# First layer's up projections by seven products of quarters

## The chip, the cores and the metric

The kernel runs on one core of a Trainium2 chip. A core has five engines that work through their own instruction queues in order and wait for each other by semaphores: TensorE (PE in the profile, with its weight loads as PEld), VectorE (DVE), ScalarE (ACT), GpSimd (POOL) and SyncE (SP, which issues most transfers). PE multiplies matrices and writes to PSUM banks; the other engines read PSUM or SBUF; POOL works on SBUF alone. The metric is the device time of one execution in microseconds; lower is better.

## The reference

The reference computes two layers on x of shape (2, 512, 512). Cut to what matters here:

```python
# layer 0, on xn = layernorm(x)
f = rfft(xn); corr = irfft(f * conj(f))            # autocorrelation of each row
weights, delay = top_k(corr, 6); w = softmax(weights)
s = sum over the 6 of w * xn rotated by delay
h = relu(xn @ up_w) ** 2                           # 512 -> 1024: the up projection
shared = h @ down_w                                # 1024 -> 512
routed = ((xn @ fc1_w) @ expert_w) * (sum of top 2 of xn @ gate_w) @ fc2_w
g = silu(layernorm(shared + routed) * gamma + beta)
x = x + s * g
# layer 1: a state-space mixer with 128 heads, and a gated feed-forward from int4 weights
```

Layer 0 is about a tenth of the time; everything that the change touches lies in it.

## The kernel before

Each of the two batches is a 512 x 512 block. Its normalized rows are transposed, so that `xnT` holds features in partitions (128 partitions, 4 blocks k of features) and the 512 rows in the free dimension. For each batch b layer 0 runs these stages, which line numbers of the profile name:

- `spectrum` (L222): the halves' sum `xu` and difference `xv` (L228 on DVE, L229 on POOL; for batch 0 row by row at L267 and L268), four spectra `xf` on PE (L235), copies on DVE (L243), squares on ACT (L245), the sum of two squares on DVE (L248).
- for b = 1 the `epilogue` of batch 0 (L334): layer norm of `ff`, product with gamma on POOL (L341), sum with beta on DVE (L342), SiLU on ACT (L343), product with the aggregate on POOL (L344), update of `x1` on DVE (L345), a store issued by POOL (L346).
- the up projection, `up_to` (L357). It makes the eight tiles of h, each 128 of the 1024 outputs by 512 rows: four matmuls over k into one PSUM bank `hu` (L361), ReLU on ACT (L369), square on POOL (L370). For b = 1 three tiles are written ahead of the correlations, the other five behind them.
- the correlations `corr`, four row blocks r (L388), and for each block the softmax over the six largest: halves (L379 to L381), maximum (L399), its negation (L401), exponentials on ACT (L404, L412, L413), match-replace (L409), the difference `w` on POOL (L415), its scaling on DVE (L416), and the halves `wuv` on POOL (L418, L419).
- `xl` (L432), the transposes of the lags' weights into `wT` (L444), their spectra `wf` (L454) and products, the router and the routed part (L483, L496), the aggregate `ag` (L507), and the down projection `sh` (L522).

A Python program writes all this with a layer that tracks dependencies and sets the semaphores. Outside of the blocks marked as scheduled by hand, a scheduler orders the instructions of layer 0 on each engine. Every engine then keeps that order: an instruction that isn't ready holds up what stands behind it. Buffers go by tags. A tag with one buffer is given to the next tile when the last reader of the former is done: `xu`, `xv` and `wT` are such tags. The PSUM banks `mm` are six, taken in turn, so a seventh tile waits until the first is read out. The weights `up_sb` lie in a ring of six buffers; the loads for the second layer's first weights (L643, L644, multiplied at L647) take these buffers when they come free.

The second layer has its order written by hand. It already uses seven products in place of eight for its projections: `row_sums` (L572), `column_sums` (L564), `seven` (L586) and `product` (L603), whose matmuls all have the line L607.

Of the kernel before, what the change touches and what calls it, by code (L numbers as in the profile page):

```python
# [8 lines left out]
F32 = mybir.dt.float32  # L9
I32 = mybir.dt.int32  # L10
AF = mybir.ActivationFunctionType
ALU = mybir.AluOpType
# [3 lines left out]
P = 128  # L16
D = 512
B = 2
S = 512
T = B * S  # L20
KD = D // P
HD = D // 2
# [26 lines left out]
def fused_kernel(  # L49
# [31 lines left out]
    nc = tc.nc  # L81
# [32 lines left out]
    def ring(name, dtype=F32):  # L114
        return wring.tile([P, 4, 512], dtype, tag="w", name=name)


    hand = early.enter_context(tc.tile_pool(name="hand", bufs=1, side="right"))
# [6 lines left out]
    def bank(name, shape=(P, 512)):  # L125
        return epsum.tile(list(shape), F32, tag="mm", name=name, bufs=6)

    def features(src, dst, name):

        pt = epsum.tile([P, KD, P], F32, tag="tr", name=name, bufs=2)  # L130
        for k in range(KD):
            nc.tensor.transpose(pt[:, k, :], src[:, bass.ts(k, P)], ident)
        nc.scalar.copy(dst, pt)

    def second_features(b):

        t = hand.tile([P, KD, S], F32, tag=f"xnT{b}", name=f"xn1T{b}")
        for r in range(NCH):
            rt = b * NCH + r
            features(acc[rt], t[:, :, bass.ts(r, P)], f"xn1t{rt}")  # L140
        return t

    x1s = ExitStack()
    x1p = x1s.enter_context(tc.tile_pool(name="x1", bufs=1, side="right"))
# [5 lines left out]
    with ExitStack() as l0:  # L150
        keep = l0.enter_context(tc.tile_pool(name="l0", bufs=1, side="left"))
# [12 lines left out]
        first = (0, HD, 1, HD + 1)  # L164
# [8 lines left out]
        up_sb = []  # L173
        for h in range(2):
            t = ring(f"up{h}")
# [10 lines left out]
        for h in range(2):  # L186
            t = ring(f"dn{h}")
# [28 lines left out]
        def halved(b):  # L216

            return [
                keep.tile([P, 2, S], F32, tag=tag, name=f"{tag}{b}") for tag in ("xu", "xv")
            ]  # L220
# [69 lines left out]
        with tc.manual_schedule():  # L290
            mv = keep.tile([P, NCH, 2], F32, tag="mv", name="mva0", bufs=2)
            rs = keep.tile([P, NCH], F32, tag="rs", name="rsa0", bufs=2)
            xu, xv = halved(0)
# [40 lines left out]
        def epilogue(b, fl, ags):  # L334

            mv, rs = stats(fl, f"f{b}")
            for r in range(NCH):
                rt = b * NCH + r
                f = fl[r]
                normed(f, f, mv, rs, r)  # L340
                nc.gpsimd.tensor_tensor(f, f, gam, ALU.mult)  # L341
                nc.vector.tensor_tensor(f, f, bet, ALU.add)  # L342
                nc.scalar.activation(f, f, AF.Silu)  # L343
                nc.gpsimd.tensor_tensor(f, f, ags[r], ALU.mult)  # L344
                nc.vector.tensor_tensor(x1[rt], x1[rt], f, ALU.add)  # L345
                nc.gpsimd.dma_start(x1_d[rows(rt), :], x1[rt])  # L346
# [3 lines left out]
        for b in range(B):  # L350
            xnT = xnTs[b]
            xf, sq = spectra.pop() if spectra else spectrum(b)
            if rest:
                epilogue(b - 1, *rest)
            h_sb = []

            def up_to(n, b=b, xnT=xnT, h_sb=h_sb):  # L357
                for o in range(len(h_sb), n):
                    ps = bank(f"hu{b}{o}")
                    for k in range(KD):  # L360
                        nc.tensor.matmul(  # L361
                            ps,
                            up_sb[o // 4][:, k, bass.ts(o % 4, P)],
                            xnT[:, k, :],
                            start=(k == 0),
                            stop=(k == KD - 1),
                        )
                    h = hand.tile([P, S], F32, tag=f"h{o}", name=f"h{b}_{o}")
                    nc.scalar.activation(h, ps, AF.Relu)  # L369
                    nc.gpsimd.tensor_tensor(h, h, h, ALU.mult)  # L370
                    h_sb.append(h)

            if rest:
                up_to(3)

            def halves(dst, ps, name):

# [7 lines left out]
            for r in range(NCH):  # L385
                ps = bank(f"corr{b}{r}")
                for c in range(3):
# [4 lines left out]
                        start=(c != 1),  # L392
                        stop=(c != 0),
# [20 lines left out]
                w = keep.tile([P, D], F32, tag="w", name=f"w{b}_{r}", bufs=2)  # L414
# [14 lines left out]
            for o in range(2):  # L429
                ps = bank(f"xl{b}{o}")  # L430
                for k in range(KD):
# [4 lines left out]
                        start=(k == 0),  # L436
                        stop=(k == KD - 1),
                    )
                nc.vector.tensor_copy(xl[:, o, :], ps)
            if b > 0:  # L440
                xn1T.append(second_features(b - 1))


            wT = keep.tile([P, KD, S], F32, tag="wT", name=f"wT{b}")  # L444
# [3 lines left out]
            for lo in range(2):  # L448
                wf = {}
                re, im = 2 * lo, 2 * lo + 1  # L450
                for c in (re, im):
                    ps = bank(f"wf{b}{c}")
                    for k in range(2):
# [4 lines left out]
                            start=(k == 0),  # L458
                            stop=(k == 1),
# [19 lines left out]
            for r in range(NCH):  # L479
                rt = b * NCH + r  # L480
                pl = bank(f"lg{rt}", (P, 8))
                for k in range(KD):
# [4 lines left out]
                        start=(k == 0),  # L487
                        stop=(k == KD - 1),
# [10 lines left out]
                f = keep.tile([P, D], F32, tag=f"ff{r}", name=f"ff{rt}")  # L499
# [3 lines left out]
            for r in range(NCH):  # L503
                rt = b * NCH + r
                ps = bank(f"ag{rt}")
                for c in range(4):
# [4 lines left out]
                        start=(c % 2 == 0),  # L511
                        stop=(c % 2 == 1),
# [4 lines left out]
            for r in range(NCH):  # L517
                rt = b * NCH + r
                f = fl[r]
                pd = bank(f"sh{rt}")  # L520
                for o in range(INT0 // P):
# [4 lines left out]
                        start=(o == 0),  # L526
                        stop=(o == INT0 // P - 1),
# [29 lines left out]
    hT = mix.tile([P, KD, T], F32, tag="hT", name="hT")  # L557
    th = mix.tile([P, B, 4, 2, HD], F32, tag="th", name="th")

    def column_quarters(a):  # L560

        return [a[:, 2 * k : 2 * k + 2, bass.ts(j, HD)] for k in range(2) for j in range(2)]

    def column_sums(b, a):  # L564


        b11, b12, b21, b22 = column_quarters(a)
        t1, t2, t3, t4 = (th[:, b, i] for i in range(4))
        for dst, p, q in ((t1, b12, b11), (t2, b22, t1), (t3, b22, b12), (t4, b21, t2)):
            nc.gpsimd.tensor_tensor(dst, p, q, ALU.subtract)  # L570

    def row_sums(a, s1, s2, s3, s4):  # L572

        a11, a12, a21, a22 = row_quarters(a)
        for dst, p, q, op in (
            (s1, a21, a22, ALU.add),
            (s2, s1, a11, ALU.subtract),
            (s3, a11, a21, ALU.subtract),
            (s4, a12, s2, ALU.subtract),
        ):  # L580
            nc.gpsimd.tensor_tensor(dst, p, q, op)  # L581

    def row_quarters(a):
        return [a[:, 2 * k : 2 * k + 2, bass.ts(r, P)] for r in range(2) for k in range(2)]

    def seven(a, sums, columns, b):  # L586


        a11, a12, _, a22 = row_quarters(a)
        s1, s2, s3, s4 = sums  # L590
        b11, _, b21, b22 = column_quarters(columns)
        t1, t2, t3, t4 = (th[:, b, i] for i in range(4))
        return {
            1: (a11, b11),
            2: (a12, b21),
            3: (s4, b22),
            4: (a22, t4),
            5: (s1, t1),
            6: (s2, t2),
            7: (s3, t3),  # L600
        }

    def product(ps, factors, first):  # L603

        x, y = factors
        for k in range(2):
            nc.tensor.matmul(  # L607
                ps,
                x[:, k, :],
                y[:, k, :],  # L610
                start=(first and k == 0),
                stop=(k == 1),
                skip_group_check=True,
            )

    Dcol = mix.tile([P, DIN // P], F32, tag="Dcol", name="Dcol")
    cw = mix.tile([P, (DIN + 2 * NG * NST) // P, KCONV], F32, tag="cw", name="cw")
# [18 lines left out]
    with ExitStack() as l1:  # L636
# [225 lines left out]
        def pair_of_tiles(its, sums, b, name):  # L862


            f = {kind: seven(*sums[kind], xn1T[b], b) for kind in "gu"}
            ps = {kind: bank(f"p{kind}{name}", (P, 2, HD)) for kind in "gu"}
            us = {
# [6 lines left out]
            def multiply(kind, i, y=None):  # L874
                if i == 2:
                    product(y, f[kind][i], kind == "g")
                else:
                    product(ps[kind][:, int(i in (3, 5))], f[kind][i], i == 1)
# [74 lines left out]
        w = {"g": fin["g"](), "u": fin["u"]()}  # L953
# [7 lines left out]
        sums = ahead = {}  # L961
        for n, (i0, iw) in enumerate(blocks):
# [13 lines left out]
            for q, b in order:  # L976
                two, name = its[b][2 * q : 2 * q + 2], f"{i0}{q}{b}"
# [24 lines left out]
                if b == 1:  # L1002
                    sums = ahead
# [9 lines left out]
            for b in range(B):  # L1013
                for r in range(NCH):
                    rt = b * NCH + r
                    po = bank(f"pf{i0}{rt}")
                    for i in range(ni):
# [4 lines left out]
                            start=(i == 0),  # L1022
                            stop=(i == ni - 1),
# [26 lines left out]
    with ExitStack() as sm:  # L1050
# [9 lines left out]
        sums, rgs = {}, {}  # L1060
# [264 lines left out]
        class Values:  # L1325
# [3 lines left out]
            def __init__(self, s):  # L1329
                self.s = s  # L1330
                u, g, b, t, h0 = place(s)
                self.ct = g * GT + t
                w = whs[s // 2]
                self.factors = seven(w, pair_sums(w, "sh", s), hT[:, :, bass.ts(b, S)], b)
                self.ps = {}

            def multiply(self, *which):
                for i in which:
                    tile = int(i not in (2, 3))
                    if i in (1, 2):  # L1340
                        self.ps[tile] = psum.tile(
                            [P, 2, HD], F32, tag="pj", name=f"pjh{self.s + tile}", bufs=3
                        )
                    product(self.ps[tile][:, int(i in (3, 5))], self.factors[i], i in (1, 2))

            def quarter(self, i, j):
                return hid[self.s + i][:, bass.ts(j, HD)]
# [657 lines left out]
```

## Time and profile before

| | us |
|---|---|
| median of 3 runs (2237.49 to 2237.68) | 2237.58 |
| the profiled execution's own time | 2236.23 |
| its span, first to last instruction | 2234.2 |
| `hu` of batch 0 in the chain, 64 passes | 27.47 |
| `hu` of batch 1 in the chain, 24 + 40 passes | 10.30 + 17.17 |
| layer 1's first product begins | 225.36 |
| L607, two products (8 passes of 256 columns) | 1.73 |

A float32 matmul is two passes in the profile. A row of the timeline gives the start, the busy time, the engine, the line, the operation, the tile written and the tiles read, the shapes, how many instructions were merged (x8), and in brackets the idle time of the engine before it and what ended that. A row of the chain gives the start, the length, the engine, the tile and the line. The granted clock of PE was 0.998 over the span.

### The profile page before, as it was taken

To read this page: it belongs to the slowest core of one execution; us is meant where nothing else is said; L and a number is where in the kernel's file an instruction comes from. 1 tells how busy PE (TensorE), PEld (TensorE's weight loads), DVE (VectorE), ACT (ScalarE), POOL (GpSimd) and SP (SyncE) were. 2 spreads that over 40 slices of the span, in tenths; PEclk is the share of its full clock that TensorE was granted. 3 is DMA by queue.
4 is the path that set the end of the run, shared out by engine and by line. 5 is a ranking of instruction groups with operands and counts; after the bars stand their busy time and mean duration, and the time that the engine had idled before them with its cause. 6 is when DMAs were issued, how large, how long until landed. Compare 5 with 4: busy or idle time off the path is not lost.

```text
span 2234.2 us, 35459 instructions
## 1 busy us (share of the span) xinstructions
PE 2198.2 (98%) x12460; PEld 1716.8 (77%) x12460; DVE 1524.5 (68%) x2989; ACT 1297.1 (58%) x2864; POOL 1311.8 (59%) x1224
## 2 busy tenths in 40 slices
PE   8999999999999999999999999999999999999997
PEld 4545567765578888888888888888888888888876
DVE  5273577545777777777767777777777777777753
ACT  4131323214876767676767676766767676767650
POOL 4151533323566667766866585768667766866485
PEclk9999999999999999999999999999999999999999
DMA  4021266755644545344544444454545444544442
GB/s 172 1 68 65 96 227 217 245 193 189 188 144 132 160 131 166 123 133 130 180 144 148 156 135 123 133 178 131 154 138 171 123 132 123 183 136 144 158 127 95
DMA packets 195521, 323.51 MB, mean 145 GB/s; under 512 B 17680, under 2 KB 129168, under 8 KB 192912
## 3 DMA queue, kind: packets, MB, share of 16 engines
q1 hardware_dynamic: 188944, 300.28, 43.2%
q0 software_dynamic: 6400, 20.98, 2.4%
q8 instruction: 99, 1.62, 0.3%
q14 instruction: 78, 0.64, 0.1%
HBM read 294.45 MB, written 26.74 MB: 144 GB/s over the span
## 4 chain that ended last, share of the span: by engine, by line
PE 82%; DVE 8%; ACT 7%; issue 2%; DMA 0%; POOL 0%; SPq 0%; ACTq 0%; POOLq 0%; DVEq 0%
PE of L1527 13%; PE pjh L607 12%; PE gt L607 11%; PE pjbc L1139 4%; PE py L1177 4%; PE pf L1018 4%; PE py L1186 3%; PE pn L1276 3%; PE hu L361 2%; PE sh L522 2%; PE pg L607 2%; PE px L1230 2%; PE pu L607 2%; PE gt L1139 2%; PE gty L607 2%
## 5 line engine op out<-in xcount | busy, mean ns | idle before, releaser
L1301 POOL TENSOR_TENSOR eb<-CT,eb 128x768 f32<-128x768 f32 x128 | 230.2, 1820 | 339.4 <-DMA eb<-ea_d 255.5
L1254 ACT ACTIVATE cs<-cs,sl 128x128 f32<-128x128 f32 x1024 | 325.2, 391 | 0.2 <-DMA cs<-cs_d 0.2
L1158 DVE SCALAR_TENSOR_TENSOR hid<-pjh,cw,hid 128x511 f32<-128x511 f32 (+2 forms) x384 | 286.6, 746 | 42.3 <-ACT hid L1149 34.8
L1269 DVE TENSOR_TENSOR cs<-de,CB 128x512 f32<-128x512 f32 x256 | 175.5, 686 | 80.4 <-ACT de L1268 79.6
L1655 POOL TENSOR_TENSOR y<-y,sgt 128x512 f32<-128x512 f32 x124 | 175.4, 1435 | 14.8 <-ACT sgt L1410 11.8
L1177 PE MATMUL py<-cs,hc 128*64 128x128 f32 x2048 | 181.4, 277 | 0.0
L1268 ACT ACTIVATE de<-cs 128x512 f32<-128x512 f32 x256 | 154.0, 602 | 28.7 <-DVE cs L1269 22.6
L1222 POOL TENSOR_TENSOR sums<-sums,sq 128x512 f32<-128x512 f32 x110 | 140.2, 1274 | 39.4 <-ACT sq L1218 35.7
L1289 DVE SCALAR_TENSOR_TENSOR st<-st,sl,pn 128x64 f32<-128x64 f32 x512 | 108.4, 275 | 77.3 <-ACT st L1285 77.3
L1186 PE MATMUL py<-eb,st 128*64 128x128 f32 x1536 | 149.9, 274 | 0.0
L1541 DVE SCALAR_TENSOR_TENSOR acc<-of,rg,acc 128x256 f32<-128x256 f32 x192 | 92.4, 482 | 81.7 <-PE of L1527 80.8
L1177 PEld LDWEIGHTS py<-cs,hc 128*64 128x64 f32 x2048 | 122.4, 138 | 19.9 <-issue 18.1
L1206 DVE SCALAR_TENSOR_TENSOR y<-hid,Dcol,y 128x512 f32<-128x512 f32 x128 | 133.7, 1045 | 4.5
L1354 ACT COPY hid<-pjh 128x256 f32<-128x256 f32 x171 | 63.4, 371 | 126.5 <-PE pjh L607 125.9
L581 POOL TENSOR_TENSOR sw<-wg 128x256 f32<-128x256 f32 x57 | 42.2, 740 | 153.0 <-PE gt L607 152.9
L1205 DVE TENSOR_TENSOR y<-py,el 128x512 f32<-128x512 f32 x128 | 87.8, 686 | 58.5 <-PE py L1186 57.8
L1399 ACT COPY sgt<-gt 128x256 f32<-128x256 f32 x171 | 64.0, 374 | 103.1 <-PE gt L607 102.8
L607 PE MATMUL gt<-th,wg 128*128 128x256 f32 x456 | 118.7, 383 | 4.2 <-DVE sgt L1403 4.2
L1527 PE MATMUL of<-wt,y 128*128 128x256 f32 x512 | 121.3, 380 | 0.0
L607 PE MATMUL pjh<-th,wh 128*128 128x256 f32 x456 | 118.7, 383 | 1.8 <-ACT hid L1354 1.8
L1139 PE MATMUL pjbc<-hT,wbc 128*128 128x512 f32 x256 | 117.4, 593 | 2.1 <-DVE BT L1158 1.3
L1527 PE MATMUL of<-wo,s 128*128 128x256 f32 x496 | 117.9, 381 | 1.2 <-DVE acc L1541 1.2
(353 smaller groups left out, 5548.6 us busy)
## 6 DMA issues: line engine op xcount, KB each, us to landing
cs<-cs_d SPq DMA_DIRECT2D x128, 512.0 KB, 4.1
eb<-ea_d SPq DMA_DIRECT2D x256, 192.0 KB, 6.0
wh<-in_in_wT SPq DMA_DIRECT2D x64, 512.0 KB, 9.0
wg<-in_in_wT SPq DMA_DIRECT2D x64, 512.0 KB, 7.3
el<-ea_d SPq DMA_DIRECT2D x256, 128.0 KB, 7.5
wo<-wo_d SPq DMA_DIRECT2D x16, 1024.0 KB, 8.2
wop<-in_out_wT SPq DMA_DIRECT2D x39, 256.0 KB, 2.8
wo_d<-wop POOLq DMA_DIRECT2D x39, 256.0 KB, 2.8
```

The lines of the kernel that those rows point to most:

```text
L607: nc.tensor.matmul(ps, x[:, k, :], y[:, k, :], start=(first and k == 0), stop=(k == 1), skip_group_check=True,)
L1139: nc.tensor.matmul(ps, w_of(k), hT[:, k, bass.ts(b, S)], start=(k == 0), stop=(k == KD - 1))
L1158: nc.vector.scalar_tensor_tensor(dst[:, j:], ps[:, : S - j], cw[:, ct, KCONV - 1 - j : KCONV - j], dst[:, j:], ALU.mult, ALU.add,)
L1177: nc.tensor.matmul(py[bass.ts(hh, HP), bass.ts(c, P)], hc[:, c, bass.ts(hh, HP)], M[:, hh, bass.ts(c, P)], start=True, stop=(c == 0),)
L1186: nc.tensor.matmul(py[bass.ts(hh, HP), bass.ts(c, P)], st[:, c - 1, bass.ts(hh, HP)], cte[:, hh, bass.ts(c - 1, P)], start=False, stop=True,)
L1222: nc.gpsimd.tensor_tensor(sums[u], sums[u], q, ALU.add)
L1254: nc.scalar.activation(m[:, bass.ts(c, P)], m[:, bass.ts(c, P)], AF.Relu, bias=sls[g][:, 3, b * NCH + c, h0 + hh : h0 + hh + 1], scale=-1.0,)
L1268: nc.scalar.activation(pe, m, AF.Exp, scale=-1.0)
L1269: nc.vector.tensor_tensor(m, pe, CBs[s // GT].rearrange("p c i -> p (c i)"), ALU.mult)
L1301: nc.gpsimd.tensor_tensor(eb_t[s], CTs[s // GT][:, P:].unsqueeze(1).to_broadcast([P, 2, S - P]), eb_t[s], ALU.mult,)
L1527: nc.tensor.matmul(ps, x[:, k, :], y[:, k, :], start=(first and k == 0), stop=(k == 3), skip_group_check=True,)
L1655: nc.gpsimd.tensor_tensor(y_of(s), y_of(s), sgs.pop(s), ALU.mult)
```

## The change

Two tiles of the up projection are made together, as one product of 2 x 2 quarters. The weights of the two tiles (512 features by 256 outputs) are cut into quarters of 256 features by 128 outputs, `xnT` into quarters of 256 features by 256 rows. Four sums of weight quarters (`row_sums`, on POOL) and four differences of quarters of `xnT` (`difference_sums`, on POOL, once a batch) let seven products of quarters stand for the eight. The differences lie in the buffers of `xu` and `xv`, the row sums in that of `wT`, with room for two pairs.

The seven are named by number: 1 is (a11, b11), 2 is (a12, b21), 3 is (s4, b22), 4 is (a22, t4), 5 is (s1, t1), 6 is (s2, t2), 7 is (s3, t3). They accumulate in two halves of one bank (`ps`) and one bank of their own (`py`); ACT copies partial sums out between products, and DVE adds the rest. ReLU now reads SBUF. Ahead of batch 1's correlations one pair (two tiles) is written in place of three tiles. The functions are moved to the top, and layer 1 calls them with its own sums as before.

```diff
+    def difference_sums(t, columns):
+        b11, b12, b21, b22 = column_quarters(columns)
+        t1, t2, t3, t4 = t
+        for dst, p, q in ((t1, b12, b11), (t2, b22, t1), (t3, b22, b12), (t4, b21, t2)):
+            nc.gpsimd.tensor_tensor(dst, p, q, ALU.subtract)
...
-            def up_to(n, b=b, xnT=xnT, h_sb=h_sb):
-                for o in range(len(h_sb), n):
-                    ps = bank(f"hu{b}{o}")
-                    for k in range(KD):
-                        nc.tensor.matmul(
-                            ps,
-                            up_sb[o // 4][:, k, bass.ts(o % 4, P)],
-                            xnT[:, k, :],
-                            start=(k == 0),
-                            stop=(k == KD - 1),
-                        )
-                    h = hand.tile([P, S], F32, tag=f"h{o}", name=f"h{b}_{o}")
-                    nc.scalar.activation(h, ps, AF.Relu)
-                    nc.gpsimd.tensor_tensor(h, h, h, ALU.mult)
-                    h_sb.append(h)
+            def up_to(n, b=b, xnT=xnT, h_sb=h_sb, tus=tus, sws=sws):
+                if not h_sb:
+                    for q, tag in enumerate(("xu", "xv")):
+                        t = keep.tile([P, 2, 2, HD], F32, tag=tag, name=f"tu{b}_{q}")
+                        tus.extend(t[:, i] for i in range(2))
+                    difference_sums(tus, xnT)
+                    sws.append(keep.tile([P, 2, 4, 2, P], F32, tag="wT", name=f"su{b}"))
+                for o in range(len(h_sb), n, 2):
+                    w = up_sb[o // 4][:, :, bass.ds(o % 4 * P, 2 * P)]
+                    sw = [sws[0][:, o // 2 % 2, i] for i in range(4)]
+                    row_sums(w, *sw)
+                    fs = seven_of(w, sw, xnT, tus)
...
+                    ps, py = bank(f"hu{b}{o}", (P, 2, HD)), bank(f"huy{b}{o}", (P, HD))
...
+                    product(ps[:, 0], fs[1], True)
+                    product(ps[:, 1], fs[5], False)
+                    product(py, fs[2], True)
+                    nc.scalar.copy(quarter(0, 0), ps[:, 0])
+                    nc.vector.tensor_tensor(quarter(0, 0), quarter(0, 0), py, ALU.add)
+                    product(ps[:, 0], fs[6], False)
+                    nc.scalar.copy(quarter(0, 1), ps[:, 0])
+                    product(ps[:, 0], fs[7], False)
+                    nc.scalar.copy(quarter(1, 1), ps[:, 0])
+                    nc.vector.tensor_tensor(quarter(1, 1), quarter(1, 1), ps[:, 1], ALU.add)
+                    product(ps[:, 0], fs[4], False)
+                    product(ps[:, 1], fs[3], False)
+                    nc.scalar.copy(quarter(1, 0), ps[:, 0])
+                    nc.vector.tensor_tensor(quarter(0, 1), quarter(0, 1), ps[:, 1], ALU.add)
+                    for h in hs:
+                        nc.scalar.activation(h, h, AF.Relu)
+                        nc.gpsimd.tensor_tensor(h, h, h, ALU.mult)
+                        h_sb.append(h)
 
             if rest:
-                up_to(3)
+                up_to(2)
```

## The prediction

> **What bounds the kernel now.** I read the page first (busy shares, the chain that ended last), then the chain in order of time over the first 330 us, then the timelines of PE, POOL, DVE and ACT there.
>
> ```profile
> span 2234.2 us, 35459 instructions
> PE 2198.2 (98%) x12460; PEld 1716.8 (77%) x12460; DVE 1524.5 (68%) x2989; ACT 1297.1 (58%) x2864; POOL 1311.8 (59%) x1224
> PE 82%; DVE 8%; ACT 7%; issue 2%; DMA 0%; POOL 0%; SPq 0%; ACTq 0%; POOLq 0%; DVEq 0%
> ```
>
> PE is busy 98% of the span, and the chain is PE for 82%. So PE time that goes is worth its full length only where PE still waits for nobody.
>
> ```profile
> 30.45 1.73 PE corr L388 x8
> 32.18 27.47 PE hu L361 x64
> 59.64 6.87 PE xl L432 x16
> ...
> 128.33 10.30 PE hu L361 x24
> 138.63 5.18 PE corr L388 x24
> 143.81 17.17 PE hu L361 x40
> ...
> 269.92 1.73 PE pg L607 x8
> ```
>
> In the chain both up projections (hu) stand whole, without a gap: 64 passes in 27.47 us (0.429 each, 512 columns), and in the second batch 24 passes ahead of the correlations (corr) and 40 behind. The other engines' rows that matter:
>
> ```profile
> 31.27 2.36 POOL L229 TENSOR_TENSOR xv<-xnT 128x1024 f32<-128x1024 f32 x1 [12.97 <-ACT xnT L133]
> 43.42 1.04 POOL L370 TENSOR_TENSOR h<-h 128x512 f32<-128x512 f32 x1
> 250.19 1.27 POOL L570 TENSOR_TENSOR th<-xn1T,th 128x512 f32<-128x512 f32 x1
> 263.13 0.74 POOL L581 TENSOR_TENSOR sg<-w_g,sg 128x256 f32<-128x256 f32 x1
> ```
>
> ```profile
> 35.88 0.49 DVE L416 TENSOR_SCALAR w<-w,zs 128x512 f32<-128x512 f32 x1 [0.37 <-POOL w L415]
> 43.49 1.28 DVE L416 TENSOR_SCALAR w<-w,zs 128x512 f32<-128x512 f32 x1 [0.62 <-POOL w L415]
> 133.50 0.68 DVE L248 TENSOR_TENSOR sq<-sq,sq 128x512 f32<-128x512 f32 x1
> ```
>
> ```profile
> 39.77 0.30 ACT L404 ACTIVATE e<-m,nm 128x6 f32<-128x6 f32 x1 [2.21 <-DVE m L407]
> 276.00 0.37 ACT L881 COPY it<-pg 128x256 f32<-128x256 f32 x1 [2.22 <-PE pg L607]
> ```
>
> The reader is to see two things. The same DVE scaling takes 0.49 us with POOL idle and 1.28 where a POOL square runs from 43.42 to 44.46: it ends about 0.3 us after the square. So a DVE operation that works from SBUF alone waits for a POOL operation in flight, and the other way round; DVE rows that read PSUM (the 0.68 us copies at L243 beside POOL) don't. And ACT idles 2.21 us for the softmax of row block 2, which costs nothing now, since PE needs nothing from ACT in that stretch.
>
> **The change part by part.**
>
> *Fewer columns on PE.* A pair of tiles was 16 passes of 0.429 = 6.87 us; it becomes seven products of 4 passes of 256 columns, and L607's rows give 1.73 per 8, so 7 x 0.864 = 6.05. Eight pairs (four per batch): 8 x 0.82 = 6.6 us off PE.
>
> *More on the others.* Per pair four row sums on POOL (0.73, pitch 0.69), four copies on ACT (0.37), three DVE adds from PSUM (0.41, L885's rows), and ReLU from SBUF (0.63 as at L343, for 0.59). Per batch four difference sums on POOL (1.27, pitch 1.23). In all 2 x (16 x 0.69 + 4 x 1.23) = 32 us POOL, about 10 ACT, 8 DVE. No engine becomes the bound by its total. What counts is the place: three of seven products write a bank that ACT must have copied and DVE must have read, and ACT, DVE and POOL do their instructions strictly in the written order. I took that order from the changed program and walked the queues with the durations above, each DVE operation from SBUF waiting for POOL's in flight. The same walk of the kernel before starts hu at 31.9 (trace 32.0), the second hu at 127.9 (128.2) and the second layer's first product at 224.9 (225.4).
>
> *Ahead of hu, batch 0.* POOL now has eight row sums (from 18.3, when xv ends and the first half of up_w has landed) and four differences, to about 29.9. Inside that stretch DVE has the sum of squares (L248) and the four normalizations that feed the transposes which stand before hu. Two of them take 1.7 us instead of 0.5; PE waits 1.2 and 1.2 at the transposes: +2.4.
>
> *Inside hu, batch 0.* Product 7 of pair 0 needs ACT's copy of product 6. On ACT that copy stands behind the exponentials of row block 2, these wait for DVE's negated maximum, which stands behind the scaling of row block 1, which waits for POOL's subtraction at 40.2 to 41.5, itself behind a row sum of pair 2. PE is through at 40.6 and goes on at 43.0: +2.4. Then product 4 waits for DVE's add of 7 and 5, behind the scaling of row block 2 (POOL, 45.5 to 46.8): +2.0. Smaller waits +0.9. Batch 0: +7.7 - 3.3 = +4.4.
>
> *Batch 1, first wait.* Before, three hu tiles (10.3 us) covered the sum of squares, done at 134.2. Now three products (2.6 us) and two corr products stand there, so PE arrives at 135.8. The sum stands on DVE behind the epilogue of batch 0. The differences can only start when xf has read the halves whose buffers they take; two of them stand on POOL ahead of the gamma products, two more and a row sum behind these, and DVE's additions and normalization alternate with them. The walk gives 142.8: +7.0.
>
> *Batch 1, second wait.* Product 4 of pair 0 needs DVE's add into h1, queued behind the four updates of x, the last of which waits for POOL's product behind a SiLU. PE is through at 148.0, goes on at 153.9: +5.9. Three further waits, for a bank that DVE's corr halves free (2.2), an ACT copy (0.9 with the neighbour) and DVE's add of pair 1 (1.9): +5.0. Batch 1: +18.0 - 3.3 = +14.7; then about 0.3 at the later transposes.
>
> *Moved.* Batch 1's halves xu and xv (2.20 and 2.36 us, L228, L229) go from 31-35 to behind batch 0's differences, about 61; xf reads them at 121, sixty microseconds of cover. The loads of w_g and w_u wait for up_w's last readers: w_g was issued at 147.3, now about 175, w_u 164.8, now about 185 (landing about 7.4 later). Their DVE products stand before two h adds (read by sh at 217) and before the multiplications at wf (about 195, read by ag at 210): nothing, with some 5 us of cover on the latter; without it ag waits. SP's other issues are not moved against each other.
>
> *Clock.* Two idle gaps of 7.0 and 5.9 us are new; in the trace PE, once started, never idles more than about 1 us, so no row shows what follows such a gap. The nearest are the first 7 us: transposes x8 1.94 against 1.04, ext and exf likewise at about half rate, together 3.4 us lost. Bounds 0 to 3.4 each. I take 0, because PE then runs into waits that DVE and ACT end. The Trainium skill (TensorE: Matmul & The Clock Gate, "What's actually happening") speaks against the change here: after an idle window of some 3.4 us the clock is halved until PE has been busy as long. By that the sum would be 1.7 larger per gap, up to 22.8 in place of 19.4; no row of this trace shows it.
>
> *Sum.* +4.4 + 14.7 + 0.3 = +19.4. The profiled execution took 2236.2 (span 2234.2 and 2.0 around it), so 2255.6; the median of the three runs shown, 2237.58, lies 1.35 above, so **2257.0**. Behind layer 0 PE's order is unchanged and without slack, so nothing is given back. With POOL rows 10% shorter the walk gives 18.2, 20% longer 22.5; with up_w's half landing at 19 instead of 17, 20.1.
>
> **The rivals.**
>
> *The sums hide, PE gets its gain.* Place: the wait of product 7 and 4 on ACT and DVE. If the copies were answered before PE has done the other pair's products, only -6.6 is left: 2231. For it: the same seven products of layer 1 (L607) run at 0.864 without a gap at 269.9. Against: there the sums were done by 266.7 and ACT and DVE have nothing between; here the softmax stands between. It decides when all new waits together stay under 6.6 us; for 0.2% (4.5 us) under 2.1. The one wait at the sum of squares would exceed that even if POOL added nothing to it: (134.2 + shift) against an arrival 7.7 us earlier than before. 4%.
>
> *POOL and DVE don't exclude each other for the new sums.* Then the same walk with free overlap gives +8.4 (nothing ahead of hu, 1.5 for 7.0, 5.5 for 5.9, 2.2 and 0.9 after): 2246. Against: the 0.49 and 1.28 above. 13%.
>
> *The clock falls in both gaps:* up to +6.8 more, 2264. 15%.
>
> My forecast (+19.4, give or take 4 for queue latencies) 65%; slower for other reasons, a wait that I don't see, 3%.
>
> **How the numbers follow.** The range takes in the free overlap and the cooled clock: 2246 to 2264; outside it lie the hidden sums and some of the unseen, about 1 in 8. A difference of 0.2% is what a measurement of this kernel can tell. Faster 0.04, same 0.01, slower 0.95.
>
> **What would show it.** PE's hu products 0.43 per two passes, but hu no longer one piece in the chain: idle before product 7 and 4 of pair 0 put down to ACT copies and DVE adds, some 5 us in batch 0, and two gaps of 5 to 7 us between 140 and 160 put down to DVE. hu of batch 0 starts about 2.4 late. DVE normalizations at 1.2 to 1.7 us beside POOL's sums; POOL about 32 us busier; later stages the same length. I am wrong if PE shows hu without gaps, if DVE keeps 0.49 beside the sums, or if later stages grow.

## The result and the profile after

The changed kernel takes 2253.52 us (median of six runs, 2251.30 to 2254.73), the kernel before 2237.63 on the same chip: ratio 1.0071, 95% interval 1.0060 to 1.0081, 15.9 us slower. The forecast was 2257.0 with 2246 to 2264. The profiled execution took 2254.73 (2236.23 before, so +18.5). Where microseconds stand beside a ratio below, they are the ratio's share of the time of before; differences of medians are called so. The page of the profiled execution, busy times and the chain's shares:

```profile
span 2253.0 us, 35753 instructions
PE 2198.8 (98%) x12556; PEld 1736.7 (77%) x12556; DVE 1537.7 (68%) x3013; ACT 1308.5 (58%) x2897; POOL 1345.2 (60%) x1264
PE 76%; DVE 8%; ACT 6%; POOL 5%; issue 3%; DMA 2%; SPq 0%; ACTq 0%; POOLq 0%; DVEq 0%
```

POOL has 33.4 us more (forecast 32), and the chain, 82% PE before, now runs over POOL for 5%. PE itself is as busy as it was: its saving is gone in something else, which the windows below show. These are the rows of PE's timeline after, from its first spectrum to the end of layer 0, in which it had waited longest:

```profile
28.39 0.70 PE L467 MATMUL corr<-p_sb,sq 128*128 128x256 f32 x2 [0.92 <-DVE sq L302]
29.89 1.70 PE L132 MATMUL xnt<-ident,xn 128*128 128x128 f32 x8 [0.80 <-DVE xn L259]
44.58 1.97 PE L165 MATMUL hu<-tu,su 128*128 128x256 f32 x8 [2.19 <-ACT h L439]
49.91 1.10 PE L165 MATMUL hu<-tu,up 128*128 128x256 f32 x4 [1.64 <-DVE h L442]
142.56 1.22 PE L467 MATMUL corr<-p_sb,sq 128*128 128x256 f32 x2 [5.19 <-DVE sq L302]
153.23 2.05 PE L165 MATMUL hu<-tu,up 128*128 128x256 f32 x4 [3.43 <-DVE h L442]
167.59 1.13 PE L165 MATMUL huy<-xnT,up 128*128 128x256 f32 x4 [1.98 <-DVE co L460]
173.94 1.13 PE L165 MATMUL hu<-tu,up 128*128 128x256 f32 x4 [1.19 <-DVE h L442]
```

From 44.58 on, each is one of the waits that the forecast named: product 7 on an ACT copy, product 4 on a DVE add, the correlations on the sum of squares, a bank on DVE's halves. Two are shorter than forecast (5.19 for 7.0, 3.43 for 5.9). Ahead of hu the forecast had two waits of 1.2 at the transposes; one stands there (0.80), the other at batch 0's sum of squares (0.92). The first wait inside hu, on ACT, DVE and POOL:

```profile
44.08 0.35 ACT L439 COPY h<-hu 128x256 f32<-128x256 f32 x1
43.78 0.30 ACT L483 ACTIVATE e<-m,nm 128x6 f32<-128x6 f32 x1 [2.96 <-DVE m L486]
43.14 0.49 DVE L495 TENSOR_SCALAR w<-w,zs 128x512 f32<-128x512 f32 x1 [1.35 <-POOL w L494]
41.84 1.27 POOL L494 TENSOR_TENSOR w<-co,mk 128x512 f32<-128x512 f32 x1
```

Read from the top, backwards in time: the copy that product 7 needs, the exponential ahead of it on ACT, the scaling of the softmax weights that DVE does ahead of the maximum for that exponential, and POOL's subtraction that the scaling waits for.

PE is also slower for a while behind the two long gaps: four passes that take 1.03 elsewhere take 2.05 at 153.23. The stretches there, with length, PE's busy time (and its instructions), granted clock, DMA share and GB/s:

```profile
143.30:145.50 2.20, 2.20 (x7) 0.50 0.00 0
153.00:155.00 2.00, 1.77 (x4) 0.51 0.33 117
155.00:157.00 2.00, 2.00 (x7) 0.63 0.09 27
```

PE's clock is at half behind both gaps, for 3.7 and 3.2 us of its work (a fall of the clock, in what follows). It was also at half ahead of hu of batch 0 (0.54 and 0.60 from 30 to 34 us). The second long wait, in the chain in order of time:

```profile
144.85 2.90 POOL ff L398 x2
...
150.26 1.27 POOL ff L398
151.55 1.20 DVE x L399
152.75 0.34 DVE h L442
153.23 3.57 PE hu L165 x8
```

POOL's product behind SiLU, the update of x, then the add that product 4 needs: the path of the forecast. On DVE the normalizations grew beside POOL's sums:

```profile
28.26 1.94 DVE L259 TENSOR_SCALAR xn<-x,mva,rsa 128x512 f32<-128x512 f32 x2
131.13 3.80 DVE L259 TENSOR_SCALAR ff<-ff,mvf,rsf 128x512 f32<-128x512 f32 x3
139.88 1.50 DVE L259 TENSOR_SCALAR ff<-ff,mvf,rsf 128x512 f32<-128x512 f32 x1
```

The same rows before:

```profile
26.94 1.00 DVE L205 TENSOR_SCALAR xn<-x,mva,rsa 128x512 f32<-128x512 f32 x2
125.54 2.40 DVE L205 TENSOR_SCALAR ff<-ff,mvf,rsf 128x512 f32<-128x512 f32 x3
133.04 0.53 DVE L205 TENSOR_SCALAR ff<-ff,mvf,rsf 128x512 f32<-128x512 f32 x1
```

The pair ahead of the transposes took 0.50 each and takes 0.97. In batch 1 three took 0.80 each beside POOL's products with gamma (L341, 126.16 to 130.74) and take 1.27 now that the sums stand there too; the fourth goes from 0.53 to 1.50. Behind layer 0 nothing changed. The table gives the stages between PE's marks (starts of xf, hu, wf, and layer 1's first product pg), read from each version's timeline; the experiments follow below.

| | xf0 to hu0 | hu0 to wf0 | hu1 to wf1 | wf1 to pg | xf0 to pg, against before |
|---|---|---|---|---|---|
| before | 14.25 | 37.50 | 45.40 | 51.80 | |
| after | 17.66 | 39.15 | 59.06 | 51.80 | +18.7 |
| after, second execution | 16.30 | 39.63 | 59.13 | 51.79 | +17.9 |
| after, third execution | 16.39 | 39.15 | 59.01 | 51.79 | +17.4 |
| seven in batch 0 only | 18.21 | 39.15 | 45.40 | 51.79 | +5.6 |
| seven in batch 1 only | 14.21 | 37.49 | 58.17 | 51.79 | +12.7 |
| sums only | 15.53 | 37.49 | 47.15 | 51.79 | +3.0 |
| raw quarters, no sums | 14.14 | 37.90 | 52.34 | 51.80 | +7.2 |
| batch 1's sums early | 15.82 | 39.16 | 53.81 | 51.79 | +11.6 |

These stage lengths are steadier than the whole times: executions of the kernel before alone spread from 2233.8 to 2239.9. Why the stages give 1.5 to 2.8 us more than the medians (+15.9) isn't explained.

### The profile page after: what moved, and what is told of

The parts are those of the page before. It is cut to its first block, busy times and chain, and to the rows that moved or that the text cites. A ratio compares the mean times of both kernels' runs of the same rounds, so it can differ in the third digit from the quotient of the medians.

```text
span 2253.0 us, 35753 instructions
## 1 busy us (share of the span) xinstructions
PE 2198.8 (98%) x12556; PEld 1736.7 (77%) x12556; DVE 1537.7 (68%) x3013; ACT 1308.5 (58%) x2897; POOL 1345.2 (60%) x1264
## 3 DMA queue, kind: packets, MB, share of 16 engines
q8 instruction: 100, 1.64, 0.3%
## 4 chain that ended last, share of the span: by engine, by line
PE 76%; DVE 8%; ACT 6%; POOL 5%; issue 3%; DMA 2%; SPq 0%; ACTq 0%; POOLq 0%; DVEq 0%
PE of L1558 13%; PE pjh L165 11%; PE gt L165 11%; PE pjbc L1170 4%; PE pf L1049 4%; PE py L1208 4%; PE py L1217 3%; PE pn L1307 3%; PE sh L601 2%; PE pg L165 2%; PE pu L165 2%; PE px L1261 2%; PE gt L1170 2%; PE gty L165 2%; ACT cs L1285 1%
## 5 line engine op out<-in xcount | busy, mean ns | idle before, releaser
L1686 POOL TENSOR_TENSOR y<-y,sgt 128x512 f32<-128x512 f32 x124 | 175.0, 1433 | 14.4 <-ACT sgt L1441 11.4
```

The costliest lines, as they stand in the source:

```text
L1686: nc.gpsimd.tensor_tensor(y_of(s), y_of(s), sgs.pop(s), ALU.mult)
```

## The experiments

The theory was the prediction's: PE waits for ACT, DVE and POOL, whose queues stand in a fixed order, and POOL and DVE hold each other up. The rivals: the sums alone carry the loss; the copies and adds alone carry it; each pair has its price; PE's clock carries it. The scheduler orders layer 0 anew for every version, so expectations come from walks over the version's own queues.

**One batch at a time**

One version makes batch 1's tiles by the eight products of the kernel before, the other (`b == 0`) batch 0's.

```diff
+                if b == 1:
+                    for o in range(len(h_sb), n):
...
+                    return
                 if not h_sb:
```

> Seven products in batch 0 only; batch 1 makes its tiles by four matmuls into one bank as before, three of them ahead of the correlations. Queue theory (the loss is waiting for ACT, DVE and POOL in their order): hu of batch 0 starts 2.4 to 3.9 late, idles about 2 and 1 at products 7 and 4, saves 3.3: slower by 4.4 (the walk of the queues) to 5.6 (what the full change had lost by wf of batch 0), 2242 to 2243.5. Rival, the loss sits only in batch 1, where PE's clock fell: this version keeps its saving and is 3.3 faster, 2234.

> Seven products in batch 1 only. Queue theory: batch 0 is as before to the microsecond, batch 1 has the whole of its gaps: slower by 13.6 (what the full change lost between xf of batch 1 and layer 1) to 14.9 (the walk of the queues), 2251 to 2252.5, with waits of some 5 and 3.5 us and half clock behind them. If the halves of the loss depend on each other (batch 0 shifts what batch 1 collides with), the two parts alone don't add up to the full change's +15.9.

Batch 0 alone: ratio 1.0019 (1.0010 to 1.0027), +4.2. Batch 1 alone: 1.0054 (1.0041 to 1.0066), +12.1. Together 16.3, for 15.9 (17.6 between the medians; 18.3 by the stages, for 17.4 to 18.7): the two losses add up. Batch 0 is not free, so the loss isn't in batch 1 alone; the theory holds with 4.4 forecast for batch 0 and batch 1 1.5 to 2.8 below its forecast.

**The sums without the products, the products without the sums**

First the sums beside the eight products, where nobody reads them; then raw quarters in the sums' place.

```diff
+                    if o in (0, 3, 4, 6):
+                        q = (o + 1) // 2
...
+                        row_sums(up_sb[q // 2][:, :, bass.ds(q % 2 * 2 * P, 2 * P)], *sw)
```

```diff
-                    difference_sums(tus, xnT)
+                    b11, b12, b21, b22 = column_quarters(xnT)
+                    tus[:] = [b12, b22, b21, b11]
-                    row_sums(w, *sw)
+                    sw = [a21, a22, a11, a12]
```

> The eight products as before, three tiles ahead of the correlations as before, but POOL makes all row sums and differences of the change, and nobody reads them. Queue theory: POOL's longer queue and its exclusion with DVE alone cost 6 (2.2 ahead of hu of batch 0, about 2.9 and 1.0 in batch 1 where ReLU and squares come late): 2243.5; the four normalizations of batch 1 take 0.8 to 1.2 in place of 0.5. Rival A, the sums carry the whole loss and the product scheme is free: 15.9 + 6.6 = 22 slower, 2260. Rival B, the copies and adds carry it: 0, 2238.

> Seven products with their copies, adds and two tiles ahead of the correlations, but each sum is replaced by a raw quarter of the same shape and POOL makes none; h is therefore another matrix. Queue theory: the normalizations ahead of hu are 0.5 each again and hu starts on time; the waits for ACT copies and DVE adds stay, 3.9 in batch 0, then about 3.3, 4.1, 1.6 and 2.7 in batch 1: 9 slower by the walk, 2246.5. Rival A (the sums carry everything): 6.6 faster, 2231. Rival B (copies and adds carry everything): 16 slower, 2253.5.

Sums only: 1.0012 (1.0003 to 1.0021), +2.7. No sums: 1.0028 (1.0018 to 1.0037), +6.3. That the sums carry everything (22 and -6.6) is out. That the copies and adds carry everything (0 and +16) fails on the second number. The theory's 6 and 9 were each some 3 too high (2 to 3 by the stages), and the two parts don't make up the 15.9: some 7 exist only where both come together. PE's timeline of the sums alone, the longest waits inside hu, shows why they cost little there:

```profile
145.10 3.70 PE L426 MATMUL hu<-xnT,up 128*128 128x512 f32 x8 [0.64 <-ACT h L434]
149.38 14.00 PE L426 MATMUL hu<-xnT,up 128*128 128x512 f32 x32 [0.58 <-ACT h L434]
```

POOL makes the same sums there, but an eight-product tile waits only for one of six banks to come free. Without sums, PE's timeline and DVE's:

```profile
40.58 3.72 PE L165 MATMUL hu<-xnT,up 128*128 128x256 f32 x16 [1.07 <-ACT h L436]
45.19 4.61 PE L165 MATMUL hu<-xnT,up 128*128 128x256 f32 x20 [0.90 <-DVE h L439]
134.74 0.70 PE L464 MATMUL corr<-p_sb,sq 128*128 128x256 f32 x2 [2.43 <-DVE sq L302]
143.58 1.99 PE L165 MATMUL hu<-xnT,up 128*128 128x256 f32 x8 [1.71 <-DVE h L439]
```

```profile
27.05 1.00 DVE L259 TENSOR_SCALAR xn<-x,mva,rsa 128x512 f32<-128x512 f32 x2
133.55 0.53 DVE L259 TENSOR_SCALAR ff<-ff,mvf,rsf 128x512 f32<-128x512 f32 x1
```

The normalizations are as before the change (ahead of hu 0.50 each; in batch 1 2.40 for three and 0.53), hu starts on time, and the waits are still there, the four largest at about half their length (1.07 for 2.19, 0.90 for 1.64, 2.43 for 5.19, 1.71 for 3.43). So it is shown that POOL's sums hold up DVE's normalizations (ahead of hu 0.50 each without the sums, 0.97 with them, 0.91 and 0.75 with the sums alone), and the product scheme needs answers from ACT and DVE that come late even without that.

**Batch 1's sums ahead of time**

```diff
+        def sums_ahead(late):
+            t = [acc[NCH + i].rearrange("p (k j) -> p k j", k=2) for i in range(4)]
+            for i in (0, 2):
+                nc.vector.tensor_copy(t[i][:, 0, 0:1], late[:, 0:1])
+            difference_sums(t, xnTs[1])
...
+            for o in (0, 2):
+                w = up_sb[0][:, :, bass.ds(o * P, 2 * P)]
+                row_sums(w, *(made[1][:, o // 2, i] for i in range(4)))
...
+            if b == 0:
+                sums_ahead(fl[0])
```

> The full change, but batch 1's four differences (in buffers of acc that are idle then) and the row sums of its first two pairs are made by POOL during batch 0's later stages, where it has room; a DVE write of one column holds them behind the routed part. Queue theory with POOL and DVE excluding each other: batch 0 as in the full change, the wait at the sum of squares 4.0 in the walk in place of 7.0, that at product 4 4.6 in place of 5.9, the rest as it was: 4.3 less than the full change's +15.9, so 11.6 slower than before, 2249. Rival, the place of the sums doesn't matter (the waits are copies and adds behind the epilogue): +16, 2253. Rival, the sums in the epilogue are the whole of batch 1's loss: batch 1 gives -3.3, in all +2, 2239.

1.0063 (1.0050 to 1.0075), +14.1; 12.8 between the medians. That interval alone leaves both 11.6 and 16 standing; the trace doesn't. From hu to wf of batch 1 it takes 53.81 for 59.06, 5.3 less (forecast 4.3), with these rows in place of 5.19 and 3.43:

```profile
138.41 0.70 PE L485 MATMUL corr<-p_sb,sq 128*128 128x256 f32 x2 [2.77 <-DVE sq L302]
147.86 1.10 PE L165 MATMUL hu<-acc,up 128*128 128x256 f32 x4 [2.32 <-DVE h L460]
```

Not all of the 5.3 is waiting. Counted from the start of hu, PE goes on 2.4 earlier at the sum of squares and needs 1.2 less from there to product 4: 3.6, where 4.3 was forecast. The other 1.6 come behind product 4, where PE's clock is at half in the full change and stays at 1.00 here (147.86 to 160.61). Some 8 of batch 1's loss stay; the waits in the rows above, for the sum of squares and for an add, are part of them, but how far the row sums that stayed in place still lengthen these waits isn't separated.

**Half of the pairs**

Pairs that `SEVEN` doesn't list for their batch are made by the eight products of the kernel before. One version lists pairs 2 and 3 of batch 0, the other (`((), (2, 3))`) those of batch 1.

```diff
+        SEVEN = ((2, 3), ())
...
+                    if o // 2 not in SEVEN[b]:
...
+                        continue
...
-                up_to(2)
+                up_to(3)
```

> Seven products only for the last two pairs of batch 0; all other tiles by four matmuls into one bank, three tiles ahead of batch 1's correlations. Queue theory: by the time these pairs come up ACT and DVE are through with the softmax, so no wait inside hu; 1.65 are saved on PE, 2.2 are lost ahead of hu, where the sums still stand beside the normalizations: +0.5, 2237.5. Rival, each seven-product pair has its price (batch 0's +4.2 over four pairs): +2.1, 2239.

> Seven products only for the last two pairs of batch 1, three tiles by four matmuls ahead of the correlations as before. Queue theory: POOL's sums stand behind the epilogue's products and beside the softmax, so the waits move (9.0 and 3.0 at the products that need the sums, 2.9 and 1.0 for ReLU) and half as many pairs lose about as much: +15.5 by the walk; batch 1 came out 2.8 below its walk when it ran alone, so +12 to +15.5, 2249 to 2252.5. Rival, a price for each pair: half of batch 1's +12.1, +6, 2243.

The last two pairs of batch 0 alone: 0.9995 (0.9987 to 1.0004), the median 1.5 below that of before, which can't be told from no change. Inside hu PE has no wait left, and hu to wf takes 35.86 for 37.50: 1.64 saved, 0.82 a pair as forecast; 1.3 go ahead of hu (15.52 for 14.25). The last two pairs of batch 1 alone: 1.0060 (1.0047 to 1.0074), +13.4 (12.2 between the medians), as much as all four (+12.1 and 12.7). A price for each pair is out on both sides: two pairs cost nothing in one place and everything in another. PE's row and ACT's for that:

```profile
160.73 2.04 PE L165 MATMUL hu<-tu,su 128*128 128x256 f32 x4 [8.62 <-POOL h L429]
```

```profile
159.94 0.30 ACT L501 ACTIVATE e<-m,nm 128x6 f32<-128x6 f32 x1 [2.89 <-DVE m L504]
160.15 0.19 ACT L501 ACTIVATION_READ_ACCUMULATOR e<-m,nm 128x1 f32 x1
160.24 0.35 ACT L454 COPY h<-hu 128x256 f32<-128x256 f32 x1
```

The wait is 8.62, but the expectation had its cause wrong: it isn't a wait for late sums. The product needs ACT's copy (L454) of the first product, which stands behind the exponential of row block 2, which waits for DVE's maximum. The copy ends at 160.59, 0.14 before PE goes on; POOL's square, which the profile names, happens to end next to it, and the last sum that the product reads was done at 135.10. It is product 6 that waits here, but in the same way as product 7 in batch 0, four times as long: for a copy that stands on ACT behind the softmax.

**The same two pairs with the sums where POOL has room**

```diff
-                        for q, tag in enumerate(("xu", "xv")):
-                            t = keep.tile([P, 2, 2, HD], F32, tag=tag, name=f"tu{b}_{q}")
+                        t = keep.tile([P, 4, 2, HD], F32, tag="wT", name=f"tu{b}")
...
+                    if o // 2 in (3,):
...
+                            for s in [hand.tile([P, S], F32, tag=f"sq{at + q}", name=f"su{b}_{o}{q}")]
```

> As the version with the last two pairs of batch 0 alone, but the sums stand where POOL has room: the differences in the buffer of wT, so that they need not wait for xf, the row sums of pair 2 in that of xu, those of pair 3 in the buffers of the squares, which hold them behind the correlations. The walk loses 1.3 ahead of hu in place of 2.2 and has no wait inside: 0.9 less than that version's -1.5, so 2.4 faster than before, 2234.7, ratio 0.9989. If the normalizations ahead of hu had not been what that version still paid, it stays at -1.5. Rival, the early stretch decides nothing: no difference, 2237.

0.9995 (0.9986 to 1.0004), the median 1.8 below. The stretch ahead of hu shrank by 0.4 (15.08 for 15.52) in place of 0.9. It can't be told from the version before it, nor from no change, so no version here is shown to beat the kernel before. (From xf0 to pg its one profile is 0.8 us shorter than that of before, that of the version before it 0.4.)

**What an idle gap costs by itself**

```diff
+                    if rt % 2 and n in GAPS and GAPS[n][rt // 2]:
+                        nc.vector.tensor_copy(scr, gl[rt - 1][:, 0:32])
+                        for _ in range(GAPS[n][rt // 2]):
+                            nc.vector.tensor_scalar(scr, scr, 1.0, None, ALU.mult)
+                        nc.tensor.matmul(po[0:32, 0:8], scr, scr[:, 0:8], start=True, stop=True)
```

> The kernel before, with ten idle gaps put into PE's stream in the second layer, ahead of every second row block of its down projection in blocks 1 and 2 and twice in block 3: a chain of small DVE operations, started by the row block two before, feeds a matmul of 8 columns. The chains have 6, 9, 12, 15, 18, 21, 24, 28, 13 and 36 links, for gaps of about 1.5 to 5.5 us, some 33 in all. What is asked is the granted clock behind each. If the clock falls to half behind gaps from 2.4 on, as after the full change's gaps of 3.4 and 5.2 and the raw-quarter version's 2.4 but not after 2.2: about eight falls of 3.3 us at half clock, 1.6 each, time = before + gaps + 13. If only gaps of 3.4 and more count: four falls, gaps + 7. If the half clock stood there for another reason than the gap: gaps alone.

2332.31, +95.2. The gaps came out twice as long as meant, 3.90 to 10.60, 67.3 in all, so they say nothing on gaps below 3.9. But all ten are followed by half clock. The shortest, and the two stretches behind it (length; busy PE, PEld, DVE, ACT, POOL; clock, DMA share, GB/s):

```profile
404.70 0.23 PE L1022 MATMUL pf<-scr 128*32 128x8 f32 x2 [3.90 <-DVE scr L1021]
```

```profile
404.70:408.00 3.30, 3.30 (x7) 1.49 (x8) 0.00 (x0) 0.00 (x0) 0.00 (x0) 0.71 0.34 130
408.00:411.00 3.00, 3.00 (x7) 1.29 (x6) 0.70 (x2) 0.00 (x0) 0.00 (x0) 0.75 0.01 3
```

Lost there: 3.3 x 0.29 + 3.0 x 0.25 = 1.7. Over all ten, worked out in this way from the clock in such stretches, it is 1.6 to 3.2 each and 23 together; 67.3 + 23 = 90 of the 95.2; the other 5 are not assigned.

**The changed kernel twice more**

> The changed kernel once more, unaltered, for the places of half clock. If a window that runs free of the kernel decides when the clock falls, the same gaps (0.8 and 0.8 ahead of hu, 2.2 and 1.6 in batch 0, 5.2, 3.4, 2.0, 1.2 in batch 1) are followed by half clock in other places than in the first profile, and the time moves by about 1.7 with each fall more or less (2250 to 2256). If the length of a gap alone decides, the falls stand as before: ahead of hu, behind 5.2 and 3.4, none behind 2.2.

> As the run before: the changed kernel unaltered. Free window: the places of half clock differ between the executions. Length alone: they are the same.

2253.57 and 2252.76. The gaps are the same, the falls are not. At product 7 in batch 0, second execution and third:

```profile
42.27 3.65 PE L165 MATMUL hu<-tu,su 128*128 128x256 f32 x8 [2.19 <-ACT h L439]
```

```profile
42.06 1.97 PE L165 MATMUL hu<-tu,su 128*128 128x256 f32 x8 [2.19 <-ACT h L439]
```

The same 2.19 us of idleness, once followed by half clock (3.65 for 1.97) and once not; the first execution had none here either, but one ahead of hu, where these two have none. Behind 5.2 and 3.2 to 3.4 all three fall. So length alone is out.

The profiles also show the window itself. In each of them the granted clock changes only at moments that lie whole multiples of 3.41 us apart, and these moments fall elsewhere in every execution. Cut at them, the window that holds most of the gap of 2.19 in batch 0 decides:

| execution | window, us | PE busy in it | clock in the next |
|---|---|---|---|
| after | 40.41 to 43.82 | 1.98 | 1.00 |
| after, second execution | 38.85 to 42.26 | 1.24 | 0.50 |
| after, third execution | 38.29 to 41.70 | 1.59 | 1.00 |
| seven in batch 0 only | 39.34 to 42.75 | 1.83 | 1.00 |
| batch 1's sums early | 40.70 to 44.12 | 1.28 | 0.50 |

The same gap lies in one window or is shared by two. Over the first 700 us of all thirteen profiles, from 20 us on, all 24 windows at full clock with PE busy for 1.45 us or less are followed by half clock, one of the seven with 1.57 to 1.78, and none of those with more. That is the range of this kernel's first 700 us, not a rule for all work on PE: later, where PE ran matmuls of one column (ssq, L1697), the kernel before has a fall behind a window with 1.93.

## Why the prediction was right, and where it was not

- **The sum.** Forecast +19.4; the stages give +18.7, +17.9 and +17.4 in three executions, the medians +15.9. Of the 3.5 by which 2257.0 is too high, 2.6 come from the last step: it added 1.35, the distance of the profiled execution of before to its median, and the profiled execution of after lay 1.2 above its own median. Profile against profile it was +18.5. That the sum came so near is in part luck, as the terms of batch 1 show.
- **PE's saving.** 0.82 a pair, shown between hu and wf where nothing covers it (1.64 for two pairs).
- **Ahead of hu.** Forecast +2.4: 2.1 in the two executions without a fall of the clock there, 3.4 with one (4.0 in the version with seven in batch 0 only, which has a fall there too).
- **Inside hu of batch 0.** Forecast +2.0 up to wf (7.7 - 2.4 - 3.3); 1.65, 2.1 and 1.65. The waits for product 7 and 4 were 2.19 and 1.64 for 2.4 and 2.0, by the path described.
- **Batch 1.** Forecast +15.0, measured +13.7, +13.7, +13.6. The places were right, the terms not: 5.19 for 7.0, 3.43 for 5.9, 3.5 for the three further waits of 5.0. PE went on at 142.56 and 153.23, the walk had 142.8 and 153.9, but PE reached the first wait at 137.4, where the walk had 135.8: against that start, its queues behind the down projection were some 2 us too slow. New waits make up 12.0 of the stage and half clock 3.4; the saving is 3.3, and 1.5 are not assigned.
- **The clock, taken as 0.** As a statement on the clock this step failed: it fell behind both long gaps, and in one execution ahead of hu, where no gap over 1 us stood. The reason given, that PE then runs into waits that other engines end, held for the first of the falls in batch 1, as the table below shows, and for most of the one at product 7 in the second execution: that took 1.7 us of PE time (5 x 0.27 + 4 x 0.08), the wait at product 4 was 0.42 for 1.63, and hu to wf took 0.5 longer. It didn't hold ahead of hu, where the stage was 1.3 longer with a fall, nor for the second fall in batch 1: from product 4 to the end of the next long wait PE needs 14.4, 14.4 and 14.3 in the three executions, and 12.75 with batch 1's sums early, where no fall stands and the wait is the same 1.98 (13.5 with a fall and a wait of 1.21 in the version with seven in batch 1 only, where about half is covered). That puts the clock's part of the loss there at up to 1.6 us, by versions that differ in POOL's work too; the prediction put it at nothing. The clock can't carry the loss: all falls in layer 0 together took 5.2, 5.4 and 3.7 us of PE time, of +18.7, +17.9 and +17.4.
- **What made up for it.** The three further waits were 1.5 shorter than forecast, and this second fall put up to 1.6 in their place. That is the luck in the sum.
- **A row that was overlooked.** The prediction says that PE never idles more than about 1 us in the trace of before. It idles 1.49 at 2125.96 (until POOL's sums, L1222), and its clock is at half from 2128.29 to 2131.70: that trace already had a fall behind a short gap. And by the prediction's own list of chances, what lies outside its range has 7 in 100 at most, not 1 in 8.
- **POOL and DVE hold each other up.** Shown for DVE's normalizations; without it the forecast would have been +8.4. In batch 1 sums made early gave 5.3 back and all sums left out 6.7, of which 1.6 and about as much are the second fall of the clock, which neither has; with no sums hu of batch 0 started on time.
- **What moved.** The weight loads and halves cost nothing: wf1 to pg is 51.80 in both.
- **The rival that the sums hide.** Even without any sums the wait at the squares is 2.43, above the 2.1 that the forecast named as its point; the scheme lost 6.3 there.

How the first fall in batch 1 is covered, in the four executions with the full change in that batch:

| execution | PE goes on at the squares | half clock takes of PE's time | wait at product 4 | PE goes on there, after |
|---|---|---|---|---|
| after | 142.56 | 1.83 | 3.43 | 10.67 |
| after, second execution | 140.72 | 1.97 | 3.29 | 10.67 |
| after, third execution | 140.02 | 2.04 | 3.22 | 10.67 |
| seven in batch 1 only | 137.70 | 2.54 | 2.72 | 10.66 |

What the clock takes and what PE waits sum to 5.26 each time: DVE's add ends the stretch, and PE's clock only sets how much of it is waiting. At full clock the wait would have been 5.26, where 5.9 was forecast.

The Trainium skill (TensorE: Matmul & The Clock Gate, "What's actually happening") says that the halved clock comes after at least one idle window of some 3.4 us, and that the window runs free of the kernel. The free window agrees with the profiles: their clock changes at multiples of 3.41 us that lie elsewhere in every execution. That the window must be idle doesn't agree, since the clock fell behind windows in which PE was busy for up to 1.45 us, and it needs no gap of 3.4 us: of the five executions with a gap of 2.19 in batch 0 two have half clock behind it (the changed kernel's second, and the version with batch 1's sums early), and of the same five with two gaps of 0.7 to 1.1 ahead of hu two have it there (the changed kernel's first, and seven in batch 0 only).

## What to carry to other kernels

Before products are saved on a saturated engine, look for what the new scheme asks of the others within a few microseconds: a product that accumulates onto a bank just copied out waits for the whole queue in front of that copy. Two pairs cost nothing in batch 0, behind the softmax, and 12 us in batch 1, inside it, so the place decides, not the count; and sums that nobody waits for are cheap (2.7 us for all of them here), unless they hold up another engine at the wrong moment. Two profiles of one kernel can differ in where the clock is at half, so one execution's waits are not to be read to a tenth, and a wait that shrinks may only have been filled by slower work.

## What was not expected of the hardware

PE's clock can fall to half behind gaps far below 3 us, and whether it does changes from execution to execution with the same gaps (2.19 us: two executions of five). What decides in the traces is how much of the gap lies in one window of a free grid of 3.41 us: with PE busy for 1.45 us or less of a window the clock was at half in the next, 24 times of 24. In ten gaps made for it, of 3.9 us and more, it fell each time and took 1.6 to 3.2 us.
